# Six turns of normalised rows in the scan stage: from TensorE transposes to a store, four strided loads and VectorE transposes

## The chip, the cores and the metric

The kernel runs on one core of one Trainium2 chip. A core has TensorE (PE in the profile, with its weight loads PEld), VectorE (DVE), ScalarE (ACT), GpSimd (POOL) and SyncE (SP), which here only issues DMAs. Each engine works through its own list of instructions in order and waits on semaphores that other engines and DMAs raise. The metric is the device time of one execution in microseconds.

## The reference, cut to what matters

Four layers, each added to its input after a layer norm: a scan layer, a mixture of experts, an attention layer, and the mixture of experts again. The input has 8 batches of 512 tokens of 256 values, all float32. The change lies in the first layer:

```python
def _L0_attn_a_ref(x, Win, bin_, Bp, Cp, Dp, Wout, bout):
    xi = jax.nn.silu(x @ Win + bin_)
    ...
    def step(h, xt):
        h = h * DECAY + xt[:, :, None] * Bp[None, :, :]
        y = jnp.einsum('bij,ji->bi', h, Cp) + Dp * xt
        return (h, y)
    ...
    return y @ Wout + bout
x = x + _L0_attn_a_ref(_layernorm(x, axis=-1), ...)
x = x + _L0_ffn_ref(_layernorm(x, axis=-1), ...)
```

The mixture (`_L0_ffn_ref`) scores 16 experts for each token, takes 4 of them, and adds two shared experts that every token passes through.

## The kernel before, in words

There are four stages: scan (batches 0 to 7), routed experts, attention (batches 0 to 7), routed experts again. The change touches the scan stage, which takes about the first 300 us of the span.

A stretch of the scan stage, the loop over `b` in `stretch`, does the work of three batches side by side: the scan layer itself of batch `b`, the norm, routing and row sends of batch `b - 1` with the shared experts of batch `b - 2`, and the norm and turn of batch `b + 1`. `timed` gives each step of the last two a place in the stretch, as a share of it, and `beside` merges the pieces by these shares. The order on each engine comes out of that and is fixed in the program.

The scan layer of a batch (`Scan.main`) begins with `pz`, the product of the normalised rows with `w_in` (L529). TensorE contracts over partitions, so it needs these rows turned: `xn`, with tokens on partitions, becomes `xT`, with the 256 values on partitions. ScalarE and VectorE make the gate and the scan of `pz` (L538 to L545), then `py` is the output product (L483), and VectorE adds it to `x` (L492).

The turn has two forms. `turned` makes eight TensorE transposes of 128 by 128 (L403) into PSUM and copies them out in two halves (L405, by ScalarE in the scan stage). `by_shares` stores the rows to a DRAM tile `through` (L413), loads them back in four DMAs (L416), each for 32 partitions and in pieces of 64 floats, and turns blocks of 32 by 32 with two VectorE transposes (L425). With `into_rows` the loads go back into the tile the rows came from. Before the change the attention stage uses `by_shares` for six turns of `xn` and six of the routing's rows; the scan stage uses `turned` throughout.

All these DMAs are issued by SP, in the order of its list. In the scan stage that list also holds the load of a later batch's `x` (L147), in five stretches the weights of two or three experts (L223 to L225, 256 KB each) with one block of zeros (L327 or L330), the store of a finished batch's `x` (L1367) and that of the shared experts' sum (L1099). GpSimd issues the row sends (L755).

VectorE's work near the end of a stretch: choices of the router (L653 to L697), statistics of the batch after next (`stats_l`, L441), the last addition to `x` (L492), statistics and `rstd` of the batch just finished (`stats_m`, L441 to L460). In the stretch of batch 2 the leftover constants (L201) stand there as well.

Of the kernel before, what the change touches and what calls it, by code (L numbers as in the profile page):

```python
# [80 lines left out]
def tile_hybrid_block(  # L81
# [257 lines left out]
    def behind(*pieces):  # L339
        def steps():  # L340
            for piece in pieces:
                yield from piece.steps

        return Piece(sum(piece.columns for piece in pieces), steps())

    def beside(*pieces):


        def steps():
            done = dict.fromkeys(range(len(pieces)), 0)  # L350
            while done:
                k = min(done, key=lambda k: done[k] / pieces[k].columns)
                step = next(pieces[k].steps, None)
                if step is None:
                    del done[k]
                else:
                    done[k] += step
                    yield step

        return Piece(sum(piece.columns for piece in pieces), steps())  # L360

    def timed(steps, *places):


        def scaled():
            now = 0
            for place in places:
                yield place - now
                now = place
                next(steps)  # L370
            for _ in steps:
                pass

        return Piece(1, scaled())

    def spread(first: float, last: float, many: int):
        return [first + (last - first) * k / many for k in range(many)]

    def some(steps, many: int):

        for _ in range(many):
            yield next(steps)

    def issue(piece):
        for _ in piece.steps:
            pass
# [4 lines left out]
    def turned(src, tag: str, into, copies, home=None, past=None):  # L391

        rows = src()
        if home is None:
            dst = work.tile([P, KD, T], FP, tag="kb4", name=f"xT_{tag}", bufs=KB)
        else:
            dst = home(f"xT_{tag}")
        into(dst)
        for k in range(KD):
            pt = bank([P, NT, P], f"pt_{tag}_{k}")  # L400
            for t in range(NT):
                with tc.issue_after(past[-1].ins) if past else nullcontext():
                    nc.tensor.transpose(pt[:, t, :], rows[:, t, :].rearrange("p (q k) -> p k q", k=KD)[:, k], ident)  # L403
            flat = pt.rearrange("p t q -> p (t q)")
            copies[k](dst[:, k, :], flat)  # L405
            yield T // 2

    def by_shares(src, tag: str, into, into_rows: bool):


        rows = src()
        through = dram.tile([T, D], FP, name=f"through_{tag}")
        nc.sync.dma_start(out=through.rearrange("(t p) d -> p t d", p=P), in_=rows)  # L413
        share = rows.rearrange("p t d -> p (t d)") if into_rows else kb4(f"share_{tag}").rearrange("p t d -> p (t d)")
        for a in range(QUAD):
            nc.sync.dma_start(  # L416
                out=share[a * SQ : (a + 1) * SQ, :].rearrange("s (g c) -> s g c", g=T // SQ),
                in_=through[:, a * KD * SQ : (a + 1) * KD * SQ].rearrange("(g s) c -> s g c", s=SQ),
            )
        yield 0  # L420
        dst = work.tile([P, KD, T], FP, tag="kb4", name=f"xT_{tag}", bufs=KB)
        into(dst)
        for half in range(2):
            g = slice(half * T // SQ // 2, (half + 1) * T // SQ // 2)
            nc.vector.transpose(  # L425
                dst.rearrange("p k (g s) -> p k g s", s=SQ)[:, :, g],
                share.rearrange("p (g i k) -> p k g i", i=SQ, k=KD)[:, :, g],
            )
        yield 0

    by_both = (nc.scalar.copy, nc.vector.tensor_copy)
    by_scalar = (nc.scalar.copy, nc.scalar.copy)
# [60 lines left out]


    class Scan:
        mixture, ahead, copies, turns = 0, 1, by_scalar, (0.75, 0.79)
        early = 0


# [615 lines left out]
    class Attention:  # L1115
        mixture, ahead, copies, turns = 1, 2, by_both, (0.65, 0.85)
# [227 lines left out]
    def stretch(layer):  # L1344


        i = layer.mixture
        xT, xn, made, routes, sends = {}, {}, {}, {}, []

        def norm(b: int, first: bool = False):  # L1350
            def place():
                xn[b] = kb4(f"xn_{i}_{b}")
                return xn[b]

            return normed(b, f"l{i}_{b}", place, first, first)

        def turn(b: int, copies=layer.copies):
            if i == 1 and b >= layer.ahead:
                return by_shares(lambda: xn.pop(b), f"l{i}_{b}", lambda xnT: xT.update({b: xnT}), True)
            return turned(lambda: xn.pop(b), f"l{i}_{b}", lambda xnT: xT.update({b: xnT}), copies)  # L1360

        def project(b: int):
            made[b], piece = layer.project(b, xT.pop(b))
            return piece
# [4 lines left out]
        def experts(b: int):  # L1369
            return shared_experts(i, b, lambda: routes.pop(b).held["xnT"], i == 1)  # L1370
# [31 lines left out]
        def start_route(b: int):  # L1402
            routes[b] = Route(i, b, layer.copies)
            store(b)
            return routes[b]
# [4 lines left out]
        for b in range(1 if begun else 0, B):  # L1410
            pieces = [begun or layer.main(b, made.pop(b))]
            begun = None
            nxt, last = b + layer.ahead, b == B - 1
            fill = []
            if layer.ahead > 1 and not last:
                fill.append(project(b + 1))
            if b > 1:
                shared_sum = experts(b - 2)
                if last:

                    each = shared_sum.columns // 12
                    rest = Piece((12 - HELD) * each, shared_sum.steps)

                    many = HELD * each if layer.mixture else HELD * each * 3 // 2
                    shared_sum = Piece(many, some(shared_sum.steps, HELD))
                fill.append(shared_sum)
                pieces.append(timed(sends.pop(), 0.1, 0.14, 0.18, *spread(0.22, 0.66 if last else 0.86, NT * TK)))
            if fill:
                pieces.append(behind(*fill))
            if b > 0:  # L1430
                r = start_route(b - 1)
                if last:
                    pieces.append(timed(r.norm(), *spread(0.0, 0.12, NT), *spread(*layer.last_rows, NT)))
                else:
                    first, then, rows, full = layer.norms
                    pieces.append(timed(r.norm(), *spread(first, then, NT), *spread(rows, full, NT)))
                sends.append(r.rest)
                if last:
                    pieces += [
                        timed(r.scores(), *layer.last_scores, *spread(0.5, 0.56, NT)),  # L1440
                        timed(some(r.rest, PICKS), *spread(0.57, 0.67, PICKS - 1), 0.76),
                        timed(some(r.rest, 3 + SENT), 0.79, 0.81, 0.83, *spread(0.85, 1.0, SENT)),
                    ]
                else:
                    pieces += [
                        timed(r.scores(i == 1), *layer.scores[:2], *spread(*layer.scores[2:], NT)),
                        timed(some(r.rest, PICKS), *spread(*layer.choose, PICKS)),
                    ]
            if nxt < B:
                added = layer.load(nxt)  # L1450
                if added is not None:
                    pieces.append(timed(added, 0.24, 0.28))
                pieces += [
                    timed(norm(nxt), *spread(0.32, 0.44, NT), *spread(0.56, 0.64, NT)),
                    timed(turn(nxt), *layer.turns),
                ]
            issue(beside(*pieces))
            if layer.ahead == 1 and nxt < B:
                issue(project(nxt))
            if i == 0 and b == 2:  # L1460
                for make in pending:
                    make()
# [25 lines left out]
    with banks_of(one=8):  # L1488
        table = stretch(Scan())
        wqkv_sb, wo_sb = load_attention_weights()  # L1490
# [6 lines left out]
    with banks_of(one=4, pair=2):  # L1497
        table = stretch(Attention())
# [128 lines left out]
```

## Time and profile before

| what | value |
|---|---|
| median of 15 runs | 1715.29 us (1709.72 to 1722.39) |
| the profiled execution's own time | 1709.48 us |
| its span | 1707.8 us |
| mean granted TensorE clock | 0.976 |
| busy: PE, DVE, ACT, POOL | 94%, 68%, 44%, 44% |
| chain that ended last: PE, DVE, DMA | 39%, 8%, 2% |

The page divides the span into 40 equal slices of 42.7 us and gives the busy share of each engine in tenths. Groups of instructions carry the line of the kernel, the engine, the operation, what it writes and reads, its count, its busy time, and the idle time in front of it with what ended it. A timeline lists instructions in order of time; neighbours of one kind are merged, and "x8" counts them.

### The profile page before, as it was taken

The page shows a single profiled execution, that of the slowest core. Times are in us where ns is not written, and L with a number is a line of the kernel's source. Part 1 is how long each engine was busy: PE and PEld are TensorE (multiplying, and loading weights), DVE is VectorE, ACT ScalarE, POOL GpSimd, SP SyncE. Part 2 cuts the span into 40 slices and gives each one's busy share as a digit, 9 for nine tenths or more (in the row PEclk, how much of TensorE's full clock was granted, in tenths as well). Part 3 has the DMA queues.
Part 4 walks back from the last instruction along what each step waited for, and adds up shares of the span by engine and source line. Part 5 has one row for each costly group of instructions (what it writes and reads, how often), then busy time and mean ns, then how long its engine had stood idle before and what let it go on. Part 6 is the DMA issues. An engine that isn't in the chain of part 4 may idle for free.

```text
span 1707.8 us, 34302 instructions
## 1 busy us (share of the span) xinstructions
PE 1605.3 (94%) x9996; PEld 1161.0 (68%) x9996; DVE 1153.9 (68%) x3693; ACT 750.3 (44%) x1494; POOL 759.6 (44%) x656
## 2 busy tenths in 40 slices
PE   6899995989999999999999999999989999999994
PEld 3566663669999999964344444444447999999993
DVE  7977875545666766657887887877853676666663
ACT  3222322125555555544554354353313555555552
POOL 3355554535555555540021431422451555555563
PEclk9999998999999999999999999998998999999997
DMA  4355422447776776641324234232544776677776
GB/s 162 117 182 174 138 81 86 166 106 109 106 104 87 126 105 99 84 84 41 84 82 119 89 95 119 77 107 73 179 156 79 105 103 97 96 139 132 129 126 178
DMA packets 278382, 192.95 MB, mean 113 GB/s; under 512 B 166992, under 2 KB 259952, under 8 KB 278192
## 3 DMA queue, kind: packets, MB, share of 16 engines
q1 hardware_dynamic: 224528, 114.68, 26.7%
q0 software_dynamic: 51984, 72.09, 24.0%
q10 hardware_dynamic: 1680, 3.93, 0.6%
q8 instruction: 85, 1.39, 0.4%
q14 instruction: 105, 0.86, 0.2%
HBM read 87.36 MB, written 103.23 MB: 112 GB/s over the span
## 4 chain that ended last, share of the span: by engine, by line
PE 39%; DVE 8%; DMA 2%; issue 2%; ACT 1%; SPq 1%; POOL 0%; ACTq 0%; POOLq 0%; DVEq 0%
PE ph L953 15%; PE pyr L984 7%; PE ps_a L1198 4%; PE pg_m L1060 3%; PE po_a L1233 3%; PE pd_m L1089 2%; PE pq_a L1143 2%; PE pv_a L1161 2%; PE py_a L483 1%; DVE w_all L1212 1%; DVE w_all L1220 1%; DMA x<-part 1%; DVE sig_m L1075 1%; DVE act_m L1076 1%; PE pt L935 1%
## 5 line engine op out<-in xcount | busy, mean ns | idle before, releaser
L994 POOL DMA_INDIRECT part<-rows x272 | 425.0, 1562 | 352.9 <-ACT rows L993 208.0
L755 POOL DMA_INDIRECT xg<-sorted_m,slots_m x256 | 260.3, 1017 | 328.2 <-ACT slots_m L752 75.1
L953 PEld LDWEIGHTS ph<-rows,gate 128*128 128x128 f32 x2160 | 279.1, 192 | 29.3 <-ACT rows L936 18.1
L953 PE MATMUL ph<-rows,gate 128*128 128x128 f32 x2160 | 291.5, 278 | 0.0
L953 PE MATMUL ph<-rows,up 128*128 128x128 f32 x2160 | 285.7, 275 | 0.0
L984 PE MATMUL pyr<-w_all,rows 128*128 x1088 | 278.9, 380 | 0.0
L926 DVE COPY up<-w_all 128x512 f32 x270 | 118.4, 439 | 218.7 <-PE ph L953 185.4
L953 PEld LDWEIGHTS ph<-rows,up 128*128 128x128 f32 x2160 | 263.4, 192 | 0.0
L926 ACT COPY gate<-w_all 128x512 f32 x270 | 166.3, 618 | 115.9 <-DVE up L926 50.1
L984 PEld LDWEIGHTS pyr<-w_all,rows 128*128 128x128 f32 x1088 | 187.0, 192 | 14.4
L993 ACT ACTIVATE rows<-pyr,gain 128x256 f32<-128x256 f32 x272 | 128.7, 473 | 80.8 <-PE pyr L984 57.2
L961 ACT ACTIVATE rows<-ph 128x256 f32<-128x256 f32 x272 | 104.3, 383 | 120.2 <-PE ph L953 95.8
L1209 ACT ACTIVATE w_all<-ps_a 128x1024 f32<-128x1024 f32 x128 | 124.4, 1020 | 55.9 <-PE ps_a L1198 46.4
L963 DVE TENSOR_TENSOR rows<-ph,rows 128x256 f32<-128x256 f32 x272 | 115.2, 424 | 43.6 <-ACT rows L961 34.0
L1198 PE MATMUL ps_a<-w_all 32*128 32x384 f32 (+3 forms) x1024 | 124.2, 476 | 11.3 <-ACT w_all L1209 8.3
L964 DVE TENSOR_TENSOR rows<-ph,rows 128x256 f32<-128x256 f32 x272 | 115.3, 424 | 25.6 <-issue 0.9
L1060 PE MATMUL pg_m<-xT_m,su_sb 128*128 128x512 f32 x256 | 125.4, 611 | 0.0
L1089 PE MATMUL pd_m<-sd_sb,act_m 128*128 128x256 f32 x512 | 122.2, 383 | 1.7 <-DVE act_m L1076 1.5
L1060 PE MATMUL pg_m<-xT_m,sg_sb 128*128 128x512 f32 x256 | 122.3, 600 | 0.0
L1089 PEld LDWEIGHTS pd_m<-sd_sb,act_m 128*128 128x128 f32 x512 | 95.4, 190 | 26.9 <-issue 7.0
L1198 PEld LDWEIGHTS ps_a<-w_all 32*128 32x128 f32 x1024 | 49.3, 186 | 80.0 <-issue 34.2
L1060 PEld LDWEIGHTS pg_m<-xT_m,sg_sb 128*128 128x128 f32 x256 | 47.1, 192 | 58.3 <-issue 50.6
(222 smaller groups left out, 2061.9 us busy)
## 6 DMA issues: line engine op xcount, KB each, us to landing
rows<-xg SPq DMA_DIRECT2D x712, 32.0 KB
rows<-xg SPq DMA_DIRECT2D x94, 134.0 KB
part<-x SPq DMA_DIRECT2D x16, 512.0 KB
part<-ys_m SPq DMA_DIRECT2D x14, 512.0 KB
sum<-part SPq DMA_DIRECT2D x13, 512.0 KB
w_all<-in_L_ffn_gate_w_dram SPq DMA_DIRECT2D x24, 256.0 KB
w_all<-in_L_ffn_up_w_dram SPq DMA_DIRECT2D x24, 256.0 KB
w_all<-in_L_ffn_down_w_dram SPq DMA_DIRECT2D x24, 256.0 KB
```

The costliest lines, as they stand in the source:

```text
L755: nc.gpsimd.indirect_dma_start(out=xg[i], out_offset=bass.IndirectOffsetOnAxis(ap=slots[:, at : at + 1], axis=0), in_=rows[:, t, :], in_of ...
L926: copy(here, w_all[:, bass.ds(held[n][0] + half * KD * F, KD * F)])
L953: nc.tensor.matmul(ph[s][:, f * P : (f + 1) * P], lhsT=both[s][:, k * F + f * P : k * F + (f + 1) * P], rhs=rows[:, ROW + k * P : ROW + (k ...
L963: nc.vector.tensor_mul(act, ph[0], act)
L964: made = nc.vector.tensor_mul(act, ph[1], act)
L984: nc.tensor.matmul(py, lhsT=act[:, f * P : (f + 1) * P], rhs=w_all[:, bass.ds(w + 2 * KD * F + f * D, D)], start=(f == 0), stop=(f == KF - 1),
L993: nc.scalar.mul(y, py, gain[:, TK : TK + 1])
L994: nc.gpsimd.indirect_dma_start(out=parts[i][n % 2], out_offset=bass.IndirectOffsetOnAxis(ap=rows[:, D + 2 * TK : D + 2 * TK + 1].bitcast(U ...
L1060: made = nc.tensor.matmul(dst, lhsT=w[:, k, f * P : (f + 1) * P], rhs=xnT[:, k, :], start=(k == 0), stop=(k == KD - 1),)
L1089: nc.tensor.matmul(py[:, j, :], lhsT=acts[n][:, f, t * P : (t + 1) * P], rhs=shared[n][3][:, f, :], start=(n == 0 and f == 0), stop=(n == ...
L1198: nc.tensor.matmul(ps[j // 2][:, j % 2, col : col + n], lhsT=k_sb[w][r, o, c * P : (c + 1) * P], rhs=q_sb[r, o, c * P : T], start=True, st ...
L1209: nc.scalar.activation(es[two], ps[two][:, :, 0:cols], AF.Exp, scale=ATT_SCALE)
```

## The change

Turns of batches 2 to 7 in the scan stage take the `by_shares` form that the attention stage has (there, `layer.ahead` is 2, so nothing changes). Their two steps get the places 0.65 (store and loads) and 0.87 (VectorE's transposes) of the stretch; the turn of batch 1 keeps TensorE and its places.

```diff
     class Scan:
-        mixture, ahead, copies, turns = 0, 1, by_scalar, (0.75, 0.79)
+        mixture, ahead, copies, turns = 0, 1, by_scalar, (0.65, 0.87)
...
         def turn(b: int, copies=layer.copies):
-            if i == 1 and b >= layer.ahead:
+            if b >= 2:
                 return by_shares(lambda: xn.pop(b), f"l{i}_{b}", lambda xnT: xT.update({b: xnT}), True)
             return turned(lambda: xn.pop(b), f"l{i}_{b}", lambda xnT: xT.update({b: xnT}), copies)
...
-                    timed(turn(nxt), *layer.turns),
+                    timed(turn(nxt), *layer.turns if nxt >= 2 else (0.75, 0.79)),
```

The function that now runs in the scan stage as well:

```python
    def by_shares(src, tag: str, into, into_rows: bool):
        rows = src()
        through = dram.tile([T, D], FP, name=f"through_{tag}")
        nc.sync.dma_start(out=through.rearrange("(t p) d -> p t d", p=P), in_=rows)
        share = rows.rearrange("p t d -> p (t d)") if into_rows else kb4(f"share_{tag}").rearrange("p t d -> p (t d)")
        for a in range(QUAD):
            nc.sync.dma_start(
                out=share[a * SQ : (a + 1) * SQ, :].rearrange("s (g c) -> s g c", g=T // SQ),
                in_=through[:, a * KD * SQ : (a + 1) * KD * SQ].rearrange("(g s) c -> s g c", s=SQ),
            )
        yield 0
        dst = work.tile([P, KD, T], FP, tag="kb4", name=f"xT_{tag}", bufs=KB)
        into(dst)
        for half in range(2):
            ...
            nc.vector.transpose(...)
        yield 0
```

## The prediction

> **What bounds the kernel now.** The first view is the page's row of busy tenths. TensorE is busy in nearly every slice; the scan stage, where the change lies, is the first seven slices (to about 300 us).
>
> ```profile
> PE   6899995989999999999999999999989999999994
> DVE  7977875545666766657887887877853676666663
> ```
>
> Next comes the table by stretch, cut where each batch's first pz_s starts: batch 3 is 101.07 to 140.10, batch 4 follows. Columns are length, then busy time of PE, weight loads, VectorE, ScalarE, GpSimd, then granted clock, DMA share and GB/s.
>
> ```profile
> 101.07:140.10 39.03, 38.19 (x150) 24.08 (x148) 32.58 (x114) 12.06 (x27) 22.17 (x24) 1.00 0.47 161
> 140.10:179.12 39.02, 38.18 (x149) 24.07 (x148) 30.87 (x96) 11.97 (x27) 21.97 (x24) 1.00 0.43 141
> ```
>
> PE fills 38.2 of 39.0 us at full clock, so whatever PE no longer does is time saved, and whatever makes PE wait is time lost. VectorE is no idle reserve: it is at 31 to 33 us. Where its work lies decides, so I read the end of one stretch (batch 4) in the timelines of both engines. Columns: start, time, engine, line.
>
> ```profile
> 171.27 1.11 PE L403 MATMUL pt_l<-ident,xn 128*128 128x128 f32 x8
> 172.22 1.89 PE L483 MATMUL py_s<-w_scan,y_s 128*128 128x256 f32 x8
> 173.94 1.89 PE L1089 MATMUL pd_m<-sd_sb,act_m 128*128 128x256 f32 x8
> 175.67 1.89 PE L483 MATMUL py_s<-w_scan,y_s 128*128 128x256 f32 x8
> 177.40 1.89 PE L1089 MATMUL pd_m<-sd_sb,act_m 128*128 128x256 f32 x8
> 179.12 1.88 PE L529 MATMUL pz_s<-xT_l,w_scan 128*128 128x512 f32 x4
> ```
>
> ```profile
> 177.60 0.69 DVE L492 TENSOR_TENSOR x<-py_s,x 128x512 f32<-128x512 f32 x1
> 178.32 0.75 DVE L441 BATCH_NORM_STATS2 stats_m<-x 128x6 f32<-128x256 f32 x2
> 178.99 0.30 DVE L442 BATCH_NORM_AGGREGATE mv_m<-stats_m 128x2 f32<-128x6 f32 x2
> 179.33 0.17 DVE L460 TENSOR_SCALAR rstd_m<-mv_m 128x4 f32<-128x4 f32 x1
> 179.41 0.16 DVE L460 TENSOR_SCALAR rstd_l<-mv_l 128x4 f32<-128x4 f32 x1
> 181.76 0.75 DVE L539 SCALAR_TENSOR_TENSOR xi_s<-pz_s,b_in_sb,xi_s 128x512 f32<-128x512 f32 x1 [2.19 <-ACT xi_s L538]
> ```
>
> Today the turn (L403) is done 7 us before pz_s needs it. VectorE works without a gap from the router's choices to 179.57, which is 0.45 us after pz_s has started; nobody minds, because pz_s waits for none of it.
>
> **What the change removes.** Turn n is the turn of batch n's rows; it runs in the stretch of batch n - 1. Per turn, eight transposes on PE and two ScalarE copies (585 ns each). The transposes hold PE from 171.27 to 172.22, 0.95 us on the path; six turns give 5.7 us. The copies lie beside PE and give nothing.
>
> **What it adds on VectorE.** Two L425 transposes a turn. The attention stage already does the same on the same shapes:
>
> ```profile
> 808.21 1.29 DVE L425 STREAM_TRANSPOSE xT_l<-xn 128x512 f32<-128x512 f32 x2
> ```
>
> The list of instructions in the built changed kernel says where they stand: in turns 4 to 7 right behind rstd (L460) of the stretch, just ahead of L539; pz_s is PE's next instruction after the last pd_m and now waits for VectorE. So the turn moves from a place with 7 us of slack to behind the tail of the norm. For turn 5 (batch 5, the stretch above): VectorE ends L460 at 179.57 as before (its tail has no idle time, so PE's earlier py_s does not pull it forward), transposes end at 180.87, pz_s starts near 180.92 instead of 179.12: +1.8 us, the 0.95 already used up. Turns 4 and 6 have the same tail (L460 ends at 140.54 and 218.60 against pz_s at 140.10 and 218.16): 3 x 1.8 = 5.4 us. In turn 7 no next batch is prepared, and VectorE waits for py_s (L492 at 255.66); that comes 0.95 earlier, L460 ends at 256.62, transposes at 257.92, pz_s at 257.97 instead of 257.19: +0.8. In turn 3 the leftover constants (L201, ending 103.20) also stand ahead of the transposes: 103.20 - 0.29 of idle before L492 + 1.35 = 104.26 against 101.07: +3.2.
>
> **What it adds on SP's queue.** One 512 KB store and four loads of 128 KB; SP runs in order, and the loads wait for the store. In the attention stage, with a quiet queue:
>
> ```profile
> 794.02 0.36 SPq L413 DMA_DIRECT2D through_l<-xn  x1
> 797.12 1.92 SPq L416 DMA_DIRECT2D xn<-through_l  x4
> ```
>
> The store takes 3.1 us until SP goes on, the loads 3.9 more (DMA is busy until 801.0): 7 us in all, of which 1.55 and 2.36 are full-width traffic. In the scan, xn is ready at 124.55 (stretch of batch 3), but SP issues weights until 127.3 and their data drains until 133.3 (DMA share 1.0). Behind that: store 1.5 to 2.3 us (GpSimd's row sends share the engines), 0.6 to complete, loads 3.9 to 5.0: landed at 139.3 to 141.2. VectorE gets to turn 4 at 140.54, so this costs 0 to 0.7; I take 0.2, since the middle of the span lies before it. Turn 3 lands by 102.3 and is covered by 102.9. Turns 5 and 6 have six weight loads instead of nine and land some 2 us earlier; turn 7 has none.
>
> Turn 2 is different. In the built list SP's next instruction after its store is the store of batch 1's x (L1367), and only then come the four loads. Before:
>
> ```profile
> 52.09 0.38 SPq L147 DMA_DIRECT2D x<-in_L_attn_a_x_dram  x1
> ...
> 58.35 0.34 SPq L327 DMA_DIRECT2D xg<-zeros  x1
> 62.08 0.38 SPq L1367 DMA_DIRECT2D part<-x  x1
> ```
>
> L1367 waits for batch 1's last addition (L492, ending 62.0, some 0.8 earlier after the change), which is the end of the very stretch. The weights drain until about 63.0, the turn's store until 64.6 and complete near 65.1; only then does SP issue the loads, whose traffic stands behind L1367's 1.5 us: landed at 69.1, transposed at 70.4, against 61.12: +9.3 us. Bounds: 8.0 if the loads' traffic overlaps the stores', 11 if it is as slow as in a shared stretch. VectorE, which in the old stretch 2 came 1.7 us late to L539 and made that stretch 0.9 longer than the others (39.95 against 39.03), has caught up by then: -0.9.
>
> Sum without the clock: 9.3 - 0.9 + 3.2 + 5.4 + 0.8 + 0.2 = 18.0 us.
>
> **The clock.** The new waits leave PE idle for about 10 us (turn 2), 4 us (turn 3), 2.6 us (4 to 6) and 1.7 us (7). What idle time does to the granted clock, by the rows (the third figure from the end is the clock):
>
> ```profile
> 285.00:286.00 1.00, 0.00 (x0) 0.00 (x0) 0.00 (x0) 0.00 (x0) 0.69 (x2) 0.78 0.29 107
> 317.00:318.00 1.00, 0.00 (x0) 0.00 (x0) 0.00 (x0) 0.30 (x1) 0.00 (x0) 1.00 0.37 137
> ```
>
> After work stopped at 283.3 the clock was halved from about 285.3, after 2.0 us; a gap of 1.7 us (around 317) left it alone; one of 3.4 us (47.8 to 51.2) halved it until 56.5. Halved stretches after the restart lasted 3.5 to 5.3 us, half of it lost, less what the 0.8 us of PE's wait for sorted_m in each stretch hides. Turn 2: 1.7, turn 3: 1.5, turns 4 to 6: 0.8 each (7 in 10 of a 1.1 us loss), turn 7: 0. Sum 5.6; bounds 0 and 16 (every wait halved for 6 us).
>
> The Trainium skill (TensorE: Matmul & The Clock Gate, Part 1) puts the return to half clock at an idle window of about 3.4 us; by that rule turns 4 to 6 would not be throttled and the sum would be 2.4 us less. The row at 285 shows the halving earlier, so I keep the row's.
>
> The Trainium skill (DMA: Bandwidth & Descriptors, Why small descriptors are slow) speaks against pieces as small as these: 256 bytes cost 11 cycles instead of 8. An estimate from that page would put the loads' traffic at 1.55 x 11/8 = 2.1 us and turn 2 at 0.2 us less. The rows show more, 2.36 us against 1.55 for the same bytes, and the rows' price is in the sum.
>
> **Sum.** 18.0 + 5.6 = 23.6 us. The profiled execution took 1709.5 us (span 1707.8), 5.8 under the median of 15 runs; on it that is 1733.1, on the median 1715.3 it is 1738.9.
>
> **Rivals.** *Faster.* The data lands in time and pz_s finds xT ready: 6 x 0.95 = 5.7 us saved, 1709.6. It decides if VectorE reaches the transposes before about 139.15 in a stretch, that is if they run ahead of the norm's tail. For it: 7 us of slack in the old order, and the attention stage does it with 1.0 us of PE waits on L425. Against: the built order, and no idle time in VectorE's tail. Chance 0.03.
> *Turn 2 is cheap.* If the x store does not hold the loads up, turn 2 ends with VectorE's choices (65.6 + 1.35 = 66.9, +5.8) or better; with less clock loss the sum is 13 to 17: 1728 to 1732. Against: the loads stand behind L1367 in the list. Chance 0.15.
> *Transfers are the bound everywhere.* If the store and the small loads take twice as long behind the weights, turns 3 to 6 land 4 us late each and PE's clock falls at each: 36 to 42 us, 1751 to 1757. For it: the DMA share of 1.0 until 133.3. Against: 0.24 from there to 140. Chance 0.13.
> That the change does something else is out: the list has 48 transposes fewer on PE, 12 more on VectorE, and nothing moved later on.
>
> **Numbers.** The forecast (waits of PE at each pz_s, worth 18 plus clock) has 0.67. 0.2% (3.4 us) is about what a measurement can tell here. Faster 0.03; within 0.2% 0.02 (several terms at their lower ends with the slack of other stages unseen by me); slower 0.95. The range goes from 1728 (turn 2 cheap, little throttling) to 1750 (clock halved at most waits).
>
> **What would show it.** pz_s waiting for DVE xT_l L425 in six places: about 9 us before batch 2, 4 before batch 3, 2.5 before batches 4 to 6, 1.7 before batch 7; stretches of 40.8 us instead of 39.0; L416 of turn 2 issued after L1367 near 65; clock rows of 0.5 behind the longer waits; the attention and expert stages unchanged in length. Wrong it would be if these waits are absent, or if a later stage gives the loss back.

## The result and the profile after

The changed kernel takes 1740.53 us (median of 9 runs, 1737.96 to 1746.98), the kernel before 1714.8 us (46 runs, 1707.79 to 1725.34): a ratio of 1.0153, 95% interval 1.0137 to 1.0170. It is 25.7 us slower. The profiled execution took 1743.0 us (span 1741.3, granted clock 0.969 against 0.976).

The page's row of PE's busy tenths: slices two to four, where the changed turns begin, fell from 8, 9, 9 to 6, 8, 8.

```profile
PE   6688998599999999998999999999897999999993
```

The table by stretch, for batches 3 and 5 (length, busy time of PE, weight loads, VectorE, ScalarE, GpSimd, then granted clock, DMA share, GB/s):

```profile
116.86:160.69 43.83, 39.18 (x141) 23.62 (x141) 32.10 (x96) 11.00 (x25) 21.33 (x23) 0.96 0.50 166
...
202.95:243.49 40.54, 37.48 (x141) 23.03 (x141) 31.73 (x96) 11.01 (x25) 22.21 (x24) 1.00 0.49 162
```

Before, these two took 39.03 and 39.04 us. The second row shows what was removed: PE is busy for 37.48 us instead of 38.2. Even so the stretch is 1.5 us longer. The first row carries a clock of 0.96 as well, as do batches 2, 4 and 6, whose stretches take 44.48, 42.26 and 41.63 us. The timeline of PE shows where the rest went (start, time, line; in brackets PE's idle time ahead and what ended it):

```profile
72.38 2.08 PE L529 MATMUL pz_s<-xT_l,w_scan 128*128 128x512 f32 x2 [12.42 <-DVE xT_l L425]
...
116.86 3.53 PE L529 MATMUL pz_s<-xT_l,w_scan 128*128 128x512 f32 x4 [4.29 <-DVE xT_l L425]
...
160.69 2.98 PE L529 MATMUL pz_s<-xT_l,w_scan 128*128 128x512 f32 x4 [3.80 <-DVE xT_l L425]
...
202.95 1.95 PE L529 MATMUL pz_s<-xT_l,w_scan 128*128 128x512 f32 x4 [2.25 <-issue]
...
243.49 3.60 PE L529 MATMUL pz_s<-xT_l,w_scan 128*128 128x512 f32 x4 [2.22 <-issue]
...
285.12 1.96 PE L529 MATMUL pz_s<-xT_l,w_scan 128*128 128x512 f32 x4 [1.67 <-DVE xT_l L425]
```

Six waits of pz_s, one per changed turn. Two are labelled "issue", but they end right behind L425 as well: the transposes begun at 242.04 take 1.30 us, and pz_s starts at 243.49. VectorE's timeline, first for turn 4, then for turn 6:

```profile
159.23 1.30 DVE L425 STREAM_TRANSPOSE xT_l<-xn 128x512 f32<-128x512 f32 x2 [1.17 <-issue]
...
241.94 0.16 DVE L460 TENSOR_SCALAR rstd_l<-mv_l 128x4 f32<-128x4 f32 x1
242.04 1.30 DVE L425 STREAM_TRANSPOSE xT_l<-xn 128x512 f32<-128x512 f32 x2
```

In turn 6 the transposes follow the norm's tail without a gap, so VectorE's list sets the wait. In turn 4 the tail's L460 ends at 158.06 and VectorE itself stands 1.17 us for the loads. SP's timeline of turns 2 and 7 tells why:

```profile
59.90 0.38 SPq L413 DMA_DIRECT2D through_l<-xn  x1
61.27 0.37 SPq L1367 DMA_DIRECT2D part<-x  x1
66.17 1.92 SPq L416 DMA_DIRECT2D xn<-through_l  x4
...
268.71 0.36 SPq L413 DMA_DIRECT2D through_l<-xn  x1
271.68 2.09 SPq L416 DMA_DIRECT2D xn<-through_l  x4
```

On a quiet queue (turn 7) the loads follow their store after 3.0 us. Behind the expert weights it takes 6.3 us (turn 2), 9.0 (turn 3, 101.03 to 110.05), 7.2 (turn 4, 146.31 to 153.53) and 7.2 to 7.9 (turns 5 and 6).

At the start of batch 7's pz_s the changed kernel is 27.9 us late (285.12 against 257.19), and 28.0 at the first py_s of the tail. The spans differ by 33.5 us. The rest lies within what single executions differ in: from batch 7's first pz_s to the end, the twelve profiled executions of this study took 1447.4 to 1463.5 us, the kernel before 1450.6, the changed one 1456.2, the fastest version below 1447.4 and 1448.0. A span of one execution is good to some 8 us here. Waits and lengths inside a stretch repeat better, starts do not: the eight executions that turn batch 2 on TensorE, with no edit ahead of it, begin batch 2's pz_s at 57.45 to 61.12 us (the kernel before at 61.12).

### The profile page after: what moved, and what is told of

Same layout as the page of the kernel before. It is cut to its first block, busy times and chain, and to the rows that moved or that the text cites. A ratio compares the mean times of both kernels' runs of the same rounds, so it can differ in the third digit from the quotient of the medians.

```text
span 1741.3 us, 34259 instructions
## 1 busy us (share of the span) xinstructions
PE 1608.1 (92%) x9948; PEld 1156.9 (66%) x9948; DVE 1159.8 (67%) x3705; ACT 744.7 (43%) x1482; POOL 760.0 (44%) x656
## 4 chain that ended last, share of the span: by engine, by line
PE 39%; DVE 6%; DMA 3%; issue 2%; POOL 1%; ACT 1%; another core or an unknown queue 0%; DVEq 0%; ACTq 0%; POOLq 0%
PE ph L953 14%; PE pyr L984 7%; PE ps_a L1198 5%; PE po_a L1233 3%; PE pg_m L1060 3%; PE pq_a L1143 3%; PE pd_m L1089 2%; PE pv_a L1161 1%; PE py_a L483 1%; DMA xg<-sorted_m,slots_m 1%; DMA part<-rows 1%; POOL xg L755 1%; DVE w_all L1212 1%; PE pt L935 1%; DVE w_all L1220 1%
## 5 line engine op out<-in xcount | busy, mean ns | idle before, releaser
L993 ACT ACTIVATE rows<-pyr,gain 128x256 f32<-128x256 f32 x272 | 128.9, 474 | 80.4 <-PE pyr L984 56.9
L529 PE MATMUL pz_s<-xT_l,w_scan 128*128 128x512 f32 x128 | 70.4, 686 | 31.0 <-DVE xT_l L425 22.2
```

The source lines that it names most:

```text
L993: nc.scalar.mul(y, py, gain[:, TK : TK + 1])
```

## The experiments

The theory: each wait belongs to its own turn, and it ends with VectorE's list or with the data, whichever is later. The rivals: only one of the two matters, or the time comes back elsewhere. Ratios are to the kernel before, run on the same chip, with 95% intervals.

**Turn 2 left out.**

```diff
-            if b >= 2:
+            if i == 1 and b >= layer.ahead or i == 0 and b >= 3:
...
-                    timed(turn(nxt), *layer.turns if nxt >= 2 else (0.75, 0.79)),
+                    timed(turn(nxt), *layer.turns if i == 1 or nxt >= 3 else (0.75, 0.79)),
```

> Turn 2 goes back to TensorE, turns 3 to 7 stay changed. Theory (the waits of pz_s add up, each belongs to its own turn): in the changed kernel's trace the first pz_s of batch 2 starts 11.3 us later than before and then runs at half clock until 76.07, which costs 1.8 us more. Both go: pz_s of batch 2 at 61.1 us, the kernel 12 to 13 us faster than the changed one, a ratio of about 1.0075 to 1.0085 to the kernel before. Rival (the later turns wait for transfers that are tied to a fixed clock, so what is won at turn 2 is waited for again at turn 3): the wait before batch 3 grows by several us and the ratio stays above 1.0115.

Measured: ratio 1.0059 (1.0033 to 1.0086), pz_s of batch 2 at 60.62 us. Batch 7's pz_s starts at 267.75, 17.4 us earlier than in the changed kernel, and the waits before batches 3 to 7 are 4.00, 2.88, 2.21, 2.20 and 1.67 us: none grew. The saving at turn 2 is kept to the end of the stage. It is more than the 12 to 13 expected because in this execution none of the waits before batches 4 to 6 halved the clock, and because turn 4's data came earlier (its wait is 2.88 instead of 3.80). The rival falls.

**Turn 2's loads ahead of the x store.**

```diff
-            nc.sync.dma_start(out=rows_of(parts[i][0], b), in_=x_tiles[b])
+            with tc.issue_after(loaded["l0_2"].ins) if (i, b) == (0, 1) else nullcontext(): nc.sync.dma_start(out=rows_of(parts[i][0], b), in_=x_tiles[b])
```

(`loaded` holds the last L416 of each turn, `laid` its last L425; `tc.issue_after` puts what stands under it behind the named instruction in its engine's list.)

> The whole change, but in the stretch of batch 1 SP issues the four loads of turn 2 (L416) ahead of the store of batch 1's x (L1367), which then waits behind them. Theory from the trace after: the loads wait for their own store, which completes at 66.1 us because its data stands behind the expert weights; L1367 was issued at 61.27, long before, and costs at most its own 1.5 us of traffic ahead of the loads. So pz_s of batch 2 starts at 70.9 to 72.4 us against 72.38, ratio 1.014 to 1.0155. Rival (the step of the prediction: SP's queue, the loads held up by L1367): without L1367 in front the loads land some 3 to 5 us sooner and VectorE's list takes over, pz_s near 67 to 69 us, ratio 1.012 to 1.013.

SP's timeline of turn 2 in this kernel, and PE's line behind it:

```profile
58.48 0.38 SPq L413 DMA_DIRECT2D through_l<-xn  x1
65.38 1.92 SPq L416 DMA_DIRECT2D xn<-through_l  x4
67.41 0.42 SPq L1367 DMA_DIRECT2D part<-x  x1
...
71.63 3.78 PE L529 MATMUL pz_s<-xT_l,w_scan 128*128 128x512 f32 x4 [11.90 <-DVE xT_l L425]
```

With nothing in between on SP's queue the loads still come 6.9 us after their store, and pz_s starts at 71.63 instead of 72.38. So L1367 was not what held the loads; the store itself was not done. Nor does L1367's traffic show: from their issue to L425 the loads take 4.9 us with it behind them (65.38 to 70.27) and 4.9 with it ahead (66.17 to 71.02). The 0.75 us need not be the edit's doing, since SP's list was already 1.1 us earlier at its load of x (L147 at 51.53 instead of 52.66). The rival falls. The ratio, 1.0183 (1.0161 to 1.0206), is no better than that of the change; it came out above the 1.014 to 1.0155 expected. The span (1742.3) and batch 7's start (285.12) are those of the changed kernel within 1 us, so what, if anything, made the median higher is not shown.

**The weights behind the loads.**

```diff
-                    for load in later[b - 1 :: shares]:
+                    for load in later[b - 1 :: shares] if b == 1 else ():
...
+        def weights(b: int):
+            with tc.issue_after(loaded[f"l0_{b}"].ins): [load() for load in later[b - 1 :: shares]]
...
-            issue(beside(*pieces))
+            issue(beside(*pieces)), weights(nxt) if i == 0 and 1 < nxt < B - 1 else None
```

> The whole change, but the weights of the experts (L223 to L225, and the zeros) that five stretches load are issued behind the four loads of the turn instead of ahead of its store. Nothing else is edited. Theory (the data of turns 2 to 4 comes late because the store stands behind the weights): the store is issued when xn is ready, completes 3.1 us later as in turn 7, and the loads land 4 to 5 us after that. Turn 2: VectorE reaches L425 at 65.5 us and no longer waits 5.5 us, pz_s near 67 instead of 72.4; turn 3: 0.2 us less; turn 4: 1.2 us less; turns 5 to 7 as they are, since VectorE's list and not the data ends their wait. Together 7 to 8 us plus up to 2 us of clock: ratio 1.0095 to 1.0115. Rival (VectorE's list alone sets every turn but the second, and the second is held by L1367): ratio 1.014 to 1.016.

SP's timeline of turn 2, and PE's line behind it:

```profile
56.34 0.36 SPq L413 DMA_DIRECT2D through_l<-xn  x1
59.30 1.92 SPq L416 DMA_DIRECT2D xn<-through_l  x4
...
66.34 3.78 PE L529 MATMUL pz_s<-xT_l,w_scan 128*128 128x512 f32 x4 [6.42 <-DVE xT_l L425]
```

The store is issued 3.6 us earlier and done 3.0 us later, as on a quiet queue. VectorE's L425 waits for no data in any turn (0.2 us in all instead of 6.9). pz_s of batch 2 starts at 66.34 instead of 72.38, and the waits are 6.42, 4.20, 2.18, 2.19, 2.53 and 2.02: turn 2 6.0 us less, turn 4 1.6 less, the others within 0.4 of the changed kernel's. Ratio 1.0098 (1.0076 to 1.0120), inside what was expected. One more thing moved with the edit: the store of x (L1367, now at 66.56) stands behind the loads too. The run before this one has it there as well, so between those two runs only the weights differ, and pz_s moves from 71.63 to 66.34. So turn 2 was held by the weights ahead of its store, and what remains is VectorE's list; the rival falls.

**Both conditions, one at a time and together (turns 3 to 7).** "Early data" is the edit above for `nxt` over 2. "Early turn" puts VectorE's transposes ahead of the last addition, and with it the norm's tail, in its list:

```diff
-            nc.vector.tensor_add(rows, py, rows)
+            with tc.issue_after(laid[f"l0_{b + 1}"].ins) if half and tag == f"s{b}" and f"l0_{b + 1}" in laid else nullcontext(): nc.vector.tensor_add(rows, py, rows)
```

> Turns 3 to 7 changed, the weights behind the loads, but VectorE's transposes left where the change has them, behind the norm's tail. Half of the faster version. Theory (VectorE's list ends these waits, and early data alone helps little): pz_s waits about 4 us before batch 3, 2.2 before batches 4 to 6, 1.7 before batch 7, as in the run without turn 2 except for 0.7 us at turn 4; ratio 1.0045 to 1.0065. Rival (late data is the loss once turn 2 is left out): the waits vanish, ratio below 1.002.

> Turns 3 to 7 changed, VectorE's transposes ahead of the last addition and the norm's tail, but the weights left ahead of the store: the other half. Theory (both conditions are needed): in turns 3 and 4 VectorE stands at L425 until the loads land, about 102.3 and 145 us, and everything behind it stands too, so nothing is won there; turn 5 wins about 0.5, turns 6 and 7, whose data comes in time, the full 2.2 and 1.7 us of the wait. About 4 us better than the run without turn 2: ratio 1.002 to 1.006. Rival (the place in VectorE's list is all that matters): ratio 0.997, as with both.

> Turns 3 to 7 changed (turn 2 on TensorE), the weights behind the loads, and VectorE's two transposes (L425) put ahead of the last addition (L492) and the norm's tail, behind the router's choice (L697). Theory (the rival called Faster, with its condition met: data there by the time and the transposes ahead of the tail): pz_s waits for nothing, each of five stretches is 0.95 us shorter than before, 38.1 instead of 39.0 us: 4.75 us, ratio 0.997. Rival (VectorE is no idle reserve: its 1.3 us more per stretch come back as later sums, statistics and sorted_m, for which TensorE waits): PE waits for sorted_m grow by about 1 us in each stretch, ratio 1.000 to 1.002.

> The faster version again, beside the others on this chip: ratio 0.996 to 0.9985 if it is a gain of 3 to 7 us; a rival that the first result was chance has it at 0.999 to 1.001.

| | transposes behind the tail | transposes ahead of it |
|---|---|---|
| weights ahead of the store | 1.0059 (1.0033 to 1.0086) | 1.0039 (1.0020 to 1.0057) |
| weights behind the loads | 1.0071 (1.0046 to 1.0096) | 0.9972 (0.9952 to 0.9993), again 0.9979 (0.9954 to 1.0004) |

Early data alone wins nothing in the time (1.0071, above the 1.0045 to 1.0065 expected, with the interval across it): pz_s waits 3.32, 2.18, 2.19, 2.13 and 1.67 us. The first two waits did shrink, from 4.00 and 2.88. But in this execution the clock was halved three times behind batch 2's pz_s (from 78.9, 102.8 and 225.7 us), in the run without turn 2 once (from 104.4), at 1.7 us each; whether that is chance or the edit is not shown. Early transposes alone move VectorE's wait to the front of its tail, as its timeline shows (turns 3 and 4):

```profile
101.82 1.30 DVE L425 STREAM_TRANSPOSE xT_l<-xn 128x512 f32<-128x512 f32 x2 [3.12 <-DMA xn<-through_l]
...
145.83 1.30 DVE L425 STREAM_TRANSPOSE xT_l<-xn 128x512 f32<-128x512 f32 x2 [3.61 <-DMA xn<-through_l]
```

Its pz_s waits are 3.51, 4.00, 1.11, 0.77 and, before batch 7, none: turn 4's grew from 2.88, as its data came later still (L425 begins 42.6 us after that stretch's first pz_s instead of 41.5). The ratio is inside the 1.002 to 1.006 expected, and the rival's 0.997 is not met. Together the loss becomes a small gain: the waits fall to 0.73, 0.40, 0.41 and 0.75, and none before batch 7. PE's wait for sorted_m stays at 0.84 us in the stretches of batches 3 to 6, so the rival that has it grow by about 1 us falls. The repeat's interval reaches 1.0004.

**The statistics behind the transposes too.** In that version `stats_l` still stood ahead of L425 (137.70, after stats_l at 136.36 and 137.10). One more edit:

```diff
-            keep(nc.vector.bn_stats(stats[:, t, :], x_sb[:, t, :]))
+            with tc.issue_after(laid[f"l0_{b - 1}"].ins) if tag == f"l0_{b}" and f"l0_{b - 1}" in laid else nullcontext(): keep(nc.vector.bn_stats(stats[:, t, :], x_sb[:, t, :]))
```

> The faster version with one more edit: the statistics of the batch after next (stats_l, L441), which stood ahead of the transposes, are put behind them too. In the faster version's trace pz_s still waits 0.4 to 0.75 us in batches 3 to 6, for transposes that end at 100.29 and 139.01. Theory: 1.2 to 1.7 us of statistics less in front of them takes these waits away, 2 to 2.5 us in all, ratio 0.9950 to 0.9965. Rival (VectorE's list has only been shifted: the first L539 of the next stretch now comes later, and TensorE waits for it or for sorted_m): ratio 0.997 to 0.999.

> The fastest version (turns 3 to 7) again, beside the one with turn 2: ratio 0.996 to 0.998 if the five stretches of 38.1 us instead of 39.0 carry through to the end; a rival that a later stage gives them back has it at 0.999 to 1.001.

The table by stretch (batch 2 in the kernel before, then batches 2 and 4 in this one) and VectorE's timeline about the beginning of batch 4:

```profile
61.12:101.07 39.95, 38.47 (x149) 24.08 (x148) 34.38 (x120) 11.31 (x26) 20.25 (x23) 1.00 0.44 154
...
59.44:100.75 41.31, 39.18 (x141) 23.83 (x140) 35.04 (x119) 10.31 (x24) 20.95 (x23) 0.96 0.39 122
...
139.07:177.15 38.08, 37.24 (x141) 23.12 (x140) 31.95 (x97) 11.00 (x25) 21.32 (x24) 1.00 0.62 193
```

```profile
136.80 1.29 DVE L425 STREAM_TRANSPOSE xT_l<-xn 128x512 f32<-128x512 f32 x2
...
141.22 0.17 DVE L460 TENSOR_SCALAR rstd_l<-mv_l 128x4 f32<-128x4 f32 x1
141.71 0.75 DVE L539 SCALAR_TENSOR_TENSOR xi_s<-pz_s,b_in_sb,xi_s 128x512 f32<-128x512 f32 x1 [0.32 <-ACT xi_s L538]
```

38.08 us instead of 39.02: the 0.95 us that the transposes took on PE, and no wait of any pz_s. Measured 0.9969 (0.9948 to 0.9991) and again 0.9970 (0.9953 to 0.9987), medians 1706.08 and 1706.28 us against 1710.61 and 1712.21. The first is a little above the 0.9950 to 0.9965 expected, where the rival has it. Of the rival's mechanism the trace shows little: L539 still waits for ScalarE (0.32 us) and not for VectorE's list, and PE's wait for sorted_m is 0.84 us as before, except in the stretches of batch 2 (1.08 and 1.05 instead of 0.43 and 1.05) and batch 3 (1.05 instead of 0.84). What fell short is turn 3. TensorE's transposes are gone from the stretch of batch 2, but that stretch takes 41.31 us instead of 39.95: the clock was halved from 81.2 to 84.6, which costs 1.7 us, and the repeat has the same (82.0 to 85.4). PE waits there for sorted_m, not at a pz_s; why the clock falls in this version and not in the kernel before is open (last section). From batch 3's pz_s to batch 7's the stage takes 152.57 us instead of 156.12, four turns' worth. It is 3.9 us ahead at batch 7, but only because batch 2 also began 1.7 us earlier, which no edit explains: its half clock near 50 us lasted one step less (last section). This version beats both kernels; its time cannot be told from that of the version without the last edit (0.9972 and 0.9979).

**Turn 2 in the fastest version.** The same edits with `b >= 2`.

> All six turns, with the weights behind the loads of each, and the transposes ahead of the statistics and the last addition: the fastest version with turn 2 added. Theory (turn 2 has no room: its xn is ready near 56 us, store and loads take 7 us even on a quiet queue, so the rows are turned near 64.7 and pz_s starts near 64.8, when PE had been done at 60): turn 2 costs 3 to 4 us against the kernel before, and 1.7 us more if the clock is halved; the other five win 0.95 each. Ratio 0.9985 to 1.0010. Rival (with the weights and the list out of the way turn 2 wins like the rest): pz_s of batch 2 near 60.2 us, ratio 0.9955 to 0.9970.

Ratio 1.0018 (1.0002 to 1.0033), some 8 us worse than without turn 2. The store is issued at 55.95, the loads at 58.91, and L425 waits for them until 64.02. pz_s starts at 65.38 after 6.73 us of idle PE, with the clock halved from 64.1 to 70.9, two windows. The rival falls. The expectation was too low because it priced turn 2 against 61.1 us and one window of half clock: the same start without turn 2 was 59.4 to 60.2.

## Why the prediction was right, step by step

The forecast was 1738.9, and the mechanism is the one foreseen: pz_s waits for L425 in all six turns. By its own terms, from the starts of pz_s, with half of each stretch of half clock behind a pz_s taken as lost:

| step | predicted | measured |
|---|---|---|
| turn 2 | +9.3 | 72.38 - 61.12 = +11.3 |
| VectorE caught up, and turn 3 | -0.9 + 3.2 = +2.3 | 44.48 - 39.95 - 1.9 (clock) = +2.6 |
| turn 4, with late data | +2.0 | 43.83 - 39.03 - 1.7 = +3.1 |
| turn 5 | +1.8 | 42.26 - 39.02 - 1.7 = +1.5 |
| turn 6 | +1.8 | 40.54 - 39.04 = +1.5 |
| turn 7 | +0.8 | 41.63 - 39.03 - 1.7 = +0.9 |
| clock | +5.6 | 1.9 + 1.7 + 1.7 + 0 + 1.7 + 0 = +7.0 |
| sum | 23.6 | 27.9 |

- Removed: PE's busy time fell from 38.2 to 37.48 us where the clock stayed full, and the fastest version shows the whole 0.95.
- VectorE's tail: right in its place, the size 0.3 too large. In the full-clock stretch before turn 6, L460 ended 39.15 us after the stretch's first pz_s instead of 39.47.
- Turn 2 was right in its main chain: the weights drain, then the store is done, "only then does SP issue the loads". What failed is the part given to L1367, "whose traffic stands behind L1367's 1.5 us": with the loads in front they took as long, 4.9 us, and pz_s moved by 0.75 us. The mis-sized terms were the store, issued at 59.90 behind the last weights and done at 66.1 instead of 65.1, and the loads, which took 4.9 us to land (71.0) instead of 4.0.
- DMA lateness in turn 4 was 1.17 us, not 0.2. The step took SP's weights at their old place, up to 26.2 us after the stretch's pz_s (127.3 - 101.07); now they were issued up to 29.4 us after it (146.2 - 116.86). The load of x ahead of them came 1.8 us later (21.1 against 19.35), about the clock's loss; one weight load then held SP for 2.09 us. Turn 3 waited 0.23, as near to covered as foreseen.
- Clock: the bounds 0 and 16 were wide, 5.6 was near 7.0. It was right to expect half clock after less than 3.4 us of idle time: turns 4 and 6 were throttled, the latter after 2.2 us of idle PE. But turn 5 was not, after the same 2.25, so going by the length of the gap was wrong, and "0.8 each (7 in 10 of a 1.1 us loss)" was in truth 1.7, 0 and 1.7. The clock of 0.78 in the row at 285 also means half clock from 285.56, 2.3 us after PE stopped, not 2.0.
- Rivals: *Faster* named its own condition rightly, and both halves of it proved needed: VectorE's list ahead of the tail and the data in time. *Turn 2 is cheap* fell: its condition held, the x store did not hold the loads up, but the turn's own store behind the weights did. With the weights out of the way pz_s starts at 66.34, near that rival's 66.9. *Transfers are the bound everywhere* was half right: store to loads did take twice as long behind the weights, but VectorE stood for it only in turns 2 to 4.
- "The later stages unchanged": they differ by less than what single executions differ in.

On the median the loss is 25.7 us, 2.1 more than the sum; in the profiled execution the scan stage lost 27.9, 4.3 more. That 1738.9 lies within 1.6 us of the measured 1740.53 is in part luck: turn 2, turn 4 and the clock were each set 1 to 2 us too low.

## What to carry to other kernels

A step moved from a busy engine to a waiting chain gains only if both ends of the chain fit: the data must land before the engine comes to it, and the step must stand in that engine's list ahead of work that nobody waits for. Two edits to order (bulk loads behind the small round trip, the transposes ahead of statistics) turned a loss of 0.6% into a gain of 0.3% with the same work. A turn whose rows are ready later than the round trip allows, 7 us on a quiet queue, stays where it was.

## What the runs showed of the hardware

The half clock comes and goes on a fixed grid, and not by the length of a gap. Behind the changed kernel's waits it began at 62.5, 117.1, 161.5 and 243.4 us and ended at 76.1, 120.5, 164.9 and 246.8: all on one grid of 3.41 us, and each but the first lasted one step. Turns 5 and 6 have the same gap, 2.25 and 2.22 us; the granted clock (third figure from the end) differs:

```profile
203.00:204.00 1.00, 1.00 (x3) 0.52 (x4) 0.00 (x0) 0.00 (x0) 0.54 (x1) 1.00 1.02 324
...
244.00:245.00 1.00, 1.00 (x2) 0.34 (x1) 0.00 (x0) 0.00 (x0) 0.08 (x1) 0.50 1.01 338
```

PE stopped at 200.70 and at 241.27. In the grid's step up to 202.4 it had been busy for 1.68 of 3.41 us (49%); in the one up to 243.4, for 1.29 (38%). In the run with turn 2's loads first it is the other way round: turn 5's step was 35% busy and halved the clock, turn 6's 70% busy and did not. In the run with early data alone, a step at 46% did not, one at 38% did. Of all steps at full clock in the first 300 us of the twelve traces that hold none of TensorE's transposes (L403), those up to 40% busy halved the clock and those from 42% on did not. So a gap of 2.2 us costs 0 or 1.7 us by where it falls.

Steps that do hold L403 do not sort this way. In the fastest version the step from 77.8 to 81.2 was 53% busy and halved the clock, 12% without L403; in the kernel before, the one from 77.4 to 80.8 was 57% busy and did not, 45% without L403. Leaving L403 out does not settle it either: in the run with early data alone the step from 48.2 to 51.6 was 54% busy, 16% without L403, and the clock stayed. What bound holds for such steps is open.

The grid lies elsewhere in each execution. The kernel before had half clock from 50.0 to 56.9, two steps, and began batch 2's pz_s at 61.12; the fastest version from 50.5 to 53.9, one step, and began it at 59.44; the run with early data alone had none there and began it at 57.45.

The Trainium skill (TensorE: Matmul & The Clock Gate, Part 1) has the window of 3.4 us, running free; the rows agree with it. It puts the half clock behind an idle window; the rows show it behind windows that were busy for over a third.
